# Graph attention on one core: other run lengths at attention's end, second parts in the step in which a run ends, and one-hot matrices of the last 60 chunks on ScalarE

## The chip, the cores and the metric

The kernel runs on one core of one Trainium2 chip, as one launch. The metric is device time in microseconds (us): the median over several executions. Beside it there is one execution taken by the hardware profiler, which has its own time. The engines are named as the profile names them: PE is TensorE (PEld its weight loads), DVE is VectorE, ACT is ScalarE, POOL is GpSimd, SP is SyncE, which here only issues DMAs.

## What is computed

A graph of 6250 nodes with 128 features and 200,000 edges, sorted by their destination. A layer norm and a rectifier, two convolutions over the edges, and then one attention over the edges, whose part is what the change touches:

```python
q = (h @ qw + qb).reshape(n, H, HD)          # H = 8 heads, HD = 16
k = (h @ kw + kb).reshape(n, H, HD)
v = (h @ vw + vb).reshape(n, H, HD)
logits = (q[dst] * k[src]).sum(-1) * scale + (edge_attr @ ew + eb)
amax = jax.ops.segment_max(logits, dst, num_segments=n)
pe = jnp.exp(logits - amax[dst])
ssum = jax.ops.segment_sum(pe, dst, num_segments=n)
w = pe / jnp.clip(ssum[dst], 1e-06)
o = jax.ops.segment_sum(w[:, :, None] * v[src], dst, num_segments=n)
o = group_norm(o.reshape(n, D) @ ow + ob, an_g, an_b)
return h + o
```

## The kernel before

**Chunks and stages.** The edges are worked in 196 chunks (`NCH`) of 8 tiles (`TPC`) of 128 edges; the last chunk has 3 tiles. The stages follow each other: a preparation, convolution 1, convolution 2, attention, and the last nodes. The change is in attention, and in `pipeline`, `early` and `second`, which the convolutions share; for them it changes only signatures.

**A chunk's first part.** `fetch` issues the loads: on SP's queue 112 rows of the table of queries into `pk` (L634) and, for two chunks at a time, the edges' relative destinations and attributes into `ohT` (L618, L621); on GpSimd's queue 8 indirect gathers (L648) of keys and values into `g`, one of 11 buffers. ScalarE turns `ohT` into a transposed one-hot matrix with a Square and a Relu (`compared`, L643 and L644). `products` multiplies it with `pk` on TensorE, 8 matmuls into `qe` (L1237), of which there is one buffer. `logits` multiplies `qe` with the gathered keys on VectorE (L1252, into `g`), reduces over each head (L1256) and adds the edges' part (L1258), which ScalarE has copied out of `qe` (L1254).

**A run.** Some chunks in a row are a run. At its end `maxima` finds the largest logit of each destination: `load_runs` has brought masks `nbs` and `nbe`, one DMA per chunk each (L1267), TensorE transposes the logits of the whole run (L1283), VectorE scans them forward and backward (L1286, L1287), TensorE transposes the result back (L1291), VectorE subtracts (L1295), ScalarE takes the exponent (L1297), and VectorE makes weights for the later maximum (L1299). `maxima` is a generator: it stops twice, so that other work stands between its pieces.

**A chunk's second part** needs its run's maxima. `onehot` compares the destinations with 0 to 127 on VectorE (L654) into `oh`, one of two buffers. `add_late` adds what the chunk before the last summed to the table (L1335 to L1341). `weighted` multiplies values and weights (L1309, the last use of the chunk's `g`) after ScalarE's copies (L1308, L1414, L1415). `sums` multiplies with the one-hot on TensorE (L1316, into one of two `us`). `merge_late` then takes up the sums of the chunk before (L1349 to L1327 on VectorE, two exponents L1329 and L1331 on ScalarE).

**Steps.** `spread` gives the lengths of the runs and `steps_of` says in which step each chunk's second part stands. In attention runs are of 8 chunks, and the last four of 6, 4, 1 and 1; a run's second parts become due in the step after the one in which it ends and are spread over the steps until the next ones are due, one or two in each. `pipeline` writes a step in this order: fetch of chunk n + 2, then `second` (with the maxima of a run that ends here between the parts of it), then `first` (the logits of chunk n), the rest of `maxima`, `compared` of chunk n + 2, `products` of chunk n + 1, `early`, and one piece of each batch of node work that is under way. Such a batch of four windows of nodes starts every 8 steps (`attention_nodes`, with rows on each engine in some 10 steps). `in_order` then fixes this order on VectorE, ScalarE, TensorE and SP; no scheduler changes it. Step 195 is the last with logits; before the change steps 196 and 197 hold the rest.

**What follows from the buffers.** With 11 buffers of `g`, the gather of chunk c + 11 waits until L1309 of chunk c is done. In runs of 8 the second part of chunk n - 9 stands in step n.

Of the kernel before, what the change touches and what calls it, by code (L numbers as in the profile page):

```python
# [8 lines left out]
FP = mybir.dt.float32  # L9
BF = mybir.dt.bfloat16  # L10
I32 = mybir.dt.int32
AF = mybir.ActivationFunctionType
ALU = mybir.AluOpType
AX = mybir.AxisListType
DVE = mybir.EngineType.DVE
# [6 lines left out]
P = 128  # L22
# [10 lines left out]
LG = 2  # L33
WN = 112
SOON = 24
KE = 5
KW = WN + KE
DB = D + H
# [9 lines left out]
def kernel(ctx: ExitStack, tc: tile.TileContext, x, src, dst, eat, w, out):  # L48
# [293 lines left out]

    def spread(i):

        sizes, n = ([1, 1, 4, 6], G) if i == 3 else ([GC] + [1] * 4, GC)
        rest, out = NCH, []
        while rest:
            out.insert(0, min(rest, sizes.pop(0) if sizes else n))
            rest -= out[0]
        return out  # L350

    def steps_of(i):


        ends, due, n = {}, {}, 0
        for m in spread(i):
            ends[n + m] = list(range(n, n + m))
            due.setdefault(n + m + (i == 3 or n < NCH - SOON), []).extend(ends[n + m])
            n += m
        waiting, todo, left = [], [], NCH  # L360
        while left:
            n = len(todo)
            waiting += due.get(n, ())
            steps = min([m for m in due if m > n], default=n + 1) - n
            k = -(-len(waiting) // steps)
            todo.append(waiting[:k])
            waiting = waiting[k:]
            left -= k
        return ends, todo
# [372 lines left out]
    def pipeline(i, stage, aside=iter(())):  # L742

        start = len(nc.cur_bb.bb.instructions)
        ends, todo = steps_of(i)  # L750
        starts = {n: j for j, (n, _) in enumerate(plans[i])}
        ahead = stage.ahead
        ks, under_way = {}, []
        for c in range(ahead):
            ks[c] = stage.fetch(c)
            compared(ks[c])
        stage.products(ks[0])
        for n, seconds in enumerate(todo):
            if n + ahead < NCH:
                ks[n + ahead] = stage.fetch(n + ahead)  # L760
            if n + 1 < NCH and stage.soon:
                stage.products(ks[n + 1])
            run = [ks[c] for c in ends.get(n, ())]
            stage.root(run)
            if n + ahead < NCH and stage.soon:
                compared(ks[n + ahead])
            stage.second(run, [ks.pop(c) for c in seconds])
            if n < NCH:
                stage.first(ks[n])
            stage.finish()  # L770
            if n + ahead < NCH and not stage.soon:
                compared(ks[n + ahead])
            if n + 1 < NCH and not stage.soon:
                stage.products(ks[n + 1])
            if n < NCH:
                stage.early(ks, n)
            if n in starts:
                for _ in aside:
                    pass
                under_way.append(stage.batch(starts[n]))  # L780
            for g in list(under_way):
                if next(g, STOP) is STOP:
                    under_way.remove(g)
            if n > 4:
                next(aside, None)
            if n < NCH:
                stage.reduce(ks[n])
        stage.flush()
        for g in (*under_way, aside):
            for _ in g:  # L790
                pass
        in_order(start)
# [111 lines left out]
    def attention_nodes(b, w, m):  # L904
# [15 lines left out]
            nc.sync.dma_start(out=hx[1][:TAIL, whole, :], in_=x[FULL * P:N, :])  # L920
        yield
        tT = b.turned(st, m)
        yield
        o = b.times(tT, m, squares["ow"])
        yield
        A = b.tile(m, "A")
# [29 lines left out]
    def with_root(b, batch):  # L956

        var = b.pool.tile([P, BN * H], FP, name="n_var")
        b.var = lambda: var
        for r in batch:  # L960
            yield
            if r == "root":
                yield from own_root(b, var, BN * H)

# [33 lines left out]
    def conv(i):  # L998
# [4 lines left out]
        with ExitStack() as es:  # L1003
# [74 lines left out]
            class Stage:  # L1078
# [23 lines left out]
                def reduce(self, k):  # L1102
                    k.reduce()

                def early(self, ks, n):

                    for k in [ks[c] for c in sorted(ks) if c <= n and ks[c].oh is None][:1]:
                        if n == NCH - 1 or k.c <= self.next:
                            onehot(k, pools, iota)
# [4 lines left out]
                        self.sd = deviations(n, self.var, NV + BN * H - n if self.roots else 0)  # L1114
                        self.j = 0

                def second(self, run, ks):
                    if run and ks and run[0].c <= ks[-1].c:
                        self.inverse(run)
                        run = []  # L1120
                    for k in ks:
                        self.next = k.c + 1
                        if k.oh is None:
                            onehot(k, pools, iota)
                        if self.late:
                            add_late(self.late.pop(0))
                        normed(k)
                        summed(k)
                        if self.sums:
                            by_window(self.sums[0])  # L1130
                            self.late.append(self.sums.pop())
                        self.sums.append(k)
                    self.inverse(run)

                def inverse(self, run):
                    if run:
# [68 lines left out]
    with ExitStack() as es:  # L1205
# [11 lines left out]
        def iota_of(k):  # L1217
            return us[k.c % 2][:, IO:IO + D // 2].bitcast(BF)
# [41 lines left out]
        def load_runs(run, bp):  # L1260

            nb = {}
            for name, d_ in (("nbs", nbs_d), ("nbe", nbe_d)):
                nb[name] = bp.tile([G * H, EPC], BF, name=name)
                for j, c in enumerate(run):
                    n = min(TPC, EI - c * TPC)
                    nc.sync.dma_start(  # L1267
                        out=nb[name][j * H:(j + 1) * H, :n * P],
                        in_=d_[c * TPC:c * TPC + n, :].rearrange("t p -> (t p)")[None, :].to_broadcast([H, n * P]))
            return nb  # L1270

        def maxima(run, lg, nb, bp):
# [83 lines left out]
        def add_late(k):  # L1356
            add(k, t3[:, bass.ds(k.win, 2), :], 2)

        class Stage:
            ahead, soon = 2, False  # L1360
            sums, late, nb = [], [], None
# [16 lines left out]
            def first(self, k):  # L1378
                if self.j == 0:
                    self.lg = wk.tile([P, TPC, G, H], FP, name="lg")  # L1380
                logits(k, self.lg[:, :, self.j, :])
                self.j += 1

            def reduce(self, k):
                pass

            def early(self, ks, n):
                pass

            def root(self, run):  # L1390
                if self.nb is None and self.runs:
                    self.nb = load_runs(self.runs.pop(0), self.bp)

            def second(self, run, ks):


                pieces = iter(())
                if run:
                    pieces = maxima(run, self.lg, self.nb, self.bp)
                    self.nb, self.j = None, 0  # L1400
                for n, k in enumerate(ks):
                    mine = pieces if n == len(ks) - 1 else iter(())
                    next(mine, None)
                    onehot(k, pools, iota_of(k))
                    if self.sums:
                        self.sums[0].win = value(w0_i, self.sums[0].c, DVE, NW - 1)
                    next(mine, None)
# [11 lines left out]
                        self.late.append(self.sums.pop())  # L1419
                    self.sums.append(k)  # L1420
                self.pieces = pieces

            def finish(self):
                for _ in self.pieces:
# [99 lines left out]
```

## Time and profile before

| what | value |
|---|---|
| median of 3 runs (lowest, highest) | 8048.32 us (8045.71, 8068.07) |
| the profiled execution: time, span | 8041.9 us, 8040.2 us |
| mean granted clock of TensorE | 0.68 |
| VectorE, GpSimd, TensorE, ScalarE busy, share of the span | 63%, 56%, 50%, 41% |
| attention: first and last start of the reduction L1256 | 5114.7, 7995.2 us |
| last add of attention ends; span ends | 8013.3, 8040.2 us |

A group's line names the source line, engine, operation, tiles written and read and count; after the bar stand busy us, the mean ns of one, then the engine's idle time just before those instructions and what ended most of it. A timeline line has the start in us, the duration, the engine, the line, the operation and the tiles; in brackets the idle time before it and what ended it. "remote" is a wait whose releaser the records don't name, "issue" is time in which the engine waited for nothing that they show.

### The profile page before, as it was taken

The numbers are of one execution on the slowest core, as the hardware profiler recorded it, in microseconds if no ns is written. First come the engines' busy times: TensorE is split into PE (matmuls) and PEld (weight loads), VectorE is DVE, ScalarE is ACT, GpSimd is POOL, SyncE is SP. The second block draws the span as 40 slices with busy tenths as digits, with TensorE's granted clock in tenths as the row PEclk, the third lists the DMA queues.
The fourth block names the chain that finished last, engine by engine and source line by source line (L and its number), as shares of the span: only waits on it lengthen the run. The fifth ranks groups of instructions, "written<-read, shape, count | busy, mean of one in ns | idle before, by whom it ended". The sixth has DMA issues, their size and how long they took to land. (4 is left out here: it accounts for less than half of the span.)

```text
span 8040.2 us, 71956 instructions
## 1 busy us (share of the span) xinstructions
PE 4000.1 (50%) x20903; PEld 3683.9 (46%) x20904; DVE 5083.1 (63%) x7387; ACT 3300.5 (41%) x5103; POOL 4484.0 (56%) x4703
## 2 busy tenths in 40 slices
PE   4555554545544454555545554254545555545544
PEld 4444444444544444445544443244444444444444
DVE  5666766666655566666766665355556556655657
ACT  4555555555544455555555544222222222222222
POOL 5666666656653666666665654445555545555552
PEclk7776667776666666766777766666666666666666
DMA  4433333333322333333333332344443444434442
GB/s 131 112 90 92 89 101 90 91 89 90 90 77 62 87 92 82 93 92 92 97 95 95 96 94 72 94 115 117 115 121 114 116 115 121 117 111 122 121 117 64
DMA packets 413748, 798.12 MB, mean 99 GB/s; under 512 B 101571, under 2 KB 274758, under 8 KB 379285
## 3 DMA queue, kind: packets, MB, share of 16 engines
q0 software_dynamic: 175056, 410.03, 19.0%
q1 hardware_dynamic: 232644, 379.76, 16.4%
q10 hardware_dynamic: 5632, 3.50, 0.2%
q8 instruction: 173, 2.83, 0.2%
q14 instruction: 243, 1.99, 0.1%
HBM read 751.94 MB, written 40.96 MB: 99 GB/s over the span
## 5 line engine op out<-in xcount | busy, mean ns | idle before, releaser
L648 POOL DMA_INDIRECT g<-b_d,src_i x3126 | 2974.6, 952 | 1931.7 <-DVE h L1041 970.1
L648 POOL DMA_INDIRECT g<-kv_d,src_i x1563 | 1488.8, 953 | 1355.0 <-DVE cm L1352 795.5
L1066 PE MATMUL u<-h,oh 128*128 128x129 f32 (+1 forms) x6252 | 1320.6, 381 | 1663.3 <-ACT h L1061 864.5
L1066 PEld LDWEIGHTS u<-h,oh 128*128 128x128 f32 x6252 | 1190.6, 285 | 1773.9 <-ACT h L1061 902.1
L1034 PE MATMUL m<-pk,ohT 117*128 117x128 f32 x6252 | 1093.3, 326 | 765.0 <-issue 722.0
L1034 PEld LDWEIGHTS m<-pk,ohT 117*128 117x128 f32 x6252 | 1008.6, 241 | 828.1 <-issue 783.4
L1041 DVE TENSOR_TENSOR h<-m,g 128x1024 f32<-128x1024 f32 x392 | 475.3, 1212 | 1058.4 <-remote 975.7
L1316 PE MATMUL us<-v,oh 128*128 128x145 f32 x3126 | 720.1, 398 | 630.4 <-issue 328.0
L1237 PE MATMUL qe<-pk,ohT 117*128 117x136 f32 x3126 | 624.6, 370 | 679.6 <-issue 394.4
L1316 PEld LDWEIGHTS us<-v,oh 128*128 128x128 f32 x3126 | 644.6, 281 | 694.2 <-issue 693.9
L1237 PEld LDWEIGHTS qe<-pk,ohT 117*128 117x128 f32 x3126 | 578.2, 271 | 726.4 <-issue 460.0
L643 ACT ACTIVATE ohT<-ohT,minus_p 112x1024 f32<-112x1024 f32 x588 | 670.5, 1140 | 35.1 <-DMA ohT<-rel_d 23.4
L1061 ACT ACTIVATE h<-h 128x1024 f32<-128x1024 f32 x392 | 412.8, 1053 | 587.7 <-DVE h L1060 292.2
L1071 ACT ACTIVATE u<-u,mask 128x129 f32<-128x129 f32 (+1 forms) x784 | 264.0, 337 | 926.5 <-remote 850.6
L644 ACT ACTIVATE ohT<-ohT 112x1024 f32<-112x1024 f32 x588 | 619.7, 1054 | 18.6
L1252 DVE TENSOR_TENSOR g<-qe,g 128x768 f32<-128x768 f32 (+1 forms) x391 | 251.8, 685 | 564.7 <-remote 439.9
L1045 DVE TENSOR_REDUCE var<-sq 128x64 f32<-128x1024 f32 x392 | 475.0, 1212 | 133.3 <-ACT u L1071 55.7
L654 DVE TENSOR_TENSOR oh<-cps,dm 128x1024 f32<-128x1024 f32 x392 | 474.4, 1210 | 96.4 <-remote 95.2
L1059 DVE TENSOR_TENSOR h<-h,cps 128x1024 f32<-128x1024 f32 x392 | 477.1, 1217 | 13.5
L1060 DVE TENSOR_TENSOR h<-h,cps 128x1024 f32<-128x1024 f32 x392 | 477.1, 1217 | 13.4
L1043 ACT ACTIVATE sq<-h 128x1024 f32<-128x1024 f32 x392 | 411.3, 1049 | 166.0 <-DVE h L1041 139.3
L1056 DVE TENSOR_TENSOR h<-h,cps 128x1024 f32<-128x1024 f32 x392 | 474.0, 1209 | 0.0
(272 smaller groups left out, 4066.4 us busy)
## 6 DMA issues: line engine op xcount, KB each, us to landing
ohT<-rel_d SPq DMA_DIRECT2D x291, 896.0 KB
g<-b_d,src_i POOLq DMA_INDIRECT x3126
pk<-a_d SPq DMA_DIRECT2D x588, 56.0 KB
g<-kv_d,src_i POOLq DMA_INDIRECT x1563
ohT<-in_eat_dram SPq DMA_DIRECT2D x291, 40.0 KB
a_d<-n_o SPq DMA_DIRECT2D x28, 256.0 KB
kv_d<-n_o SPq DMA_DIRECT2D x28, 256.0 KB
n_h<-h_d SPq DMA_DIRECT2D x19, 256.0 KB
```

The costliest lines, as they stand in the source:

```text
L643: nc.scalar.activation(k.ohT[:WN, :], k.ohT[:WN, :], AF.Square, bias=minus_p[:WN])
L644: nc.scalar.activation(k.ohT[:WN, :], k.ohT[:WN, :], AF.Relu, bias=1.0, scale=-4.0)
L648: nc.gpsimd.indirect_dma_start(out=g[:, t, :table_d.shape[1]], out_offset=None, in_=table_d, in_offset=bass.IndirectOffsetOnAxis(ap=k.src[ ...
L654: return nc.vector.tensor_tensor(k.oh[:, :k.nt, :], iota[:, None, :].to_broadcast([P, k.nt, P]), k.dm[:, :, None].to_broadcast([P, k.nt, P ...
L1034: nc.tensor.matmul(k.m[:, t, :], lhsT=lhs[:, t * P:(t + 1) * P], rhs=rhs, start=(j == 0), stop=(j == len(terms) - 1))
L1041: nc.vector.tensor_tensor(k.mt, k.m[:, :n], k.g[:, :n], ALU.add)
L1045: return lambda: nc.vector.tensor_reduce(var[:, at:at + n * H], sq[:, :n].rearrange("p t (g c) -> p (t g) c", c=HD), AX.X, ALU.add)
L1059: nc.vector.tensor_tensor(k.mt, k.mt, over_edges(gam, k.nt), ALU.mult)
L1060: nc.vector.tensor_tensor(k.mt, k.mt, over_edges(bet, k.nt), ALU.add)
L1066: nc.tensor.matmul(k.u[:, 0, :wide], lhsT=k.oh[:, t, :], rhs=k.h[:, t, :wide], start=(t == 0), stop=(t == k.nt - 1))
L1237: nc.tensor.matmul(k.qe[:, t // TB, at:at + DB], lhsT=lhs[:, t * P:(t + 1) * P], rhs=rhs, start=(j == 0), stop=(j == len(terms) - 1))
L1316: nc.tensor.matmul(k.u[:, :wide], lhsT=k.oh[:, t, :], rhs=k.v[:, t, :wide], start=(t == 0), stop=(t == k.nt - 1))
```

## The change

The last seven runs of attention become 7, 7, 6, 5, 4, 3 and 4 chunks (`TAILS`). `spread` takes the list from its back, so that 4 is the last, and 160 chunks in 20 runs of 8 stand before them. Second parts of these 36 chunks become due in the step in which their run ends instead of the one after. So steps 161 and 162 hold two second parts, and so do 174, 180 and 185, where a run ends; step 189 holds two, step 195 none and step 196 the last four; step 197 is gone. Where a run's own second parts stand in its last step (`own`), `second` writes another order: the transposes, the one-hot of the run's second chunk that stands here, the logits of chunk n (`first`), the late add, all the rest of `maxima`, and then the second parts.

For the last 60 chunks (`BY_ACT`) `early` lets ScalarE make the one-hot of the next step's first second part, as 1 - (j - d) squared, cut off below zero: 8 Squares with a bias from the destinations and one Relu (`onehot_by_act`). With the one in `own` that is 56 chunks; of the other four (153, 155, 194, 195) VectorE still makes it. VectorE's count of L654 in attention goes from 196 to 140; ScalarE gets 56 x 9 instructions.

A batch of nodes stops once with "held": if a run ends in the next step, its piece waits one step. The masks' loads are now always of a whole chunk, and a short chunk's unused logits are set to zero. The diff:

```diff
--- before.py
+++ after.py
@@ -33,6 +33,8 @@
 LG = 2
 WN = 112
 SOON = 24
+TAILS = [7, 7, 6, 5, 4, 3, 4]
+BY_ACT = 60
 KE = 5
 KW = WN + KE
 DB = D + H
@@ -342,7 +344,7 @@
 
     def spread(i):
 
-        sizes, n = ([1, 1, 4, 6], G) if i == 3 else ([GC] + [1] * 4, GC)
+        sizes, n = (TAILS[::-1], G) if i == 3 else ([GC] + [1] * 4, GC)
         rest, out = NCH, []
         while rest:
             out.insert(0, min(rest, sizes.pop(0) if sizes else n))
@@ -355,7 +357,7 @@
         ends, due, n = {}, {}, 0
         for m in spread(i):
             ends[n + m] = list(range(n, n + m))
-            due.setdefault(n + m + (i == 3 or n < NCH - SOON), []).extend(ends[n + m])
+            due.setdefault(n + m + (n < NCH - (sum(TAILS) if i == 3 else SOON)), []).extend(ends[n + m])
             n += m
         waiting, todo, left = [], [], NCH
         while left:
@@ -750,7 +752,7 @@
         ends, todo = steps_of(i)
         starts = {n: j for j, (n, _) in enumerate(plans[i])}
         ahead = stage.ahead
-        ks, under_way = {}, []
+        ks, under_way, said = {}, [], {}
         for c in range(ahead):
             ks[c] = stage.fetch(c)
             compared(ks[c])
@@ -764,22 +766,25 @@
             stage.root(run)
             if n + ahead < NCH and stage.soon:
                 compared(ks[n + ahead])
-            stage.second(run, [ks.pop(c) for c in seconds])
-            if n < NCH:
-                stage.first(ks[n])
+            first = (lambda k: lambda: stage.first(k))(ks[n]) if n < NCH else None
+            if stage.second(run, [ks.pop(c) for c in seconds], first) and first:
+                first()
             stage.finish()
             if n + ahead < NCH and not stage.soon:
                 compared(ks[n + ahead])
             if n + 1 < NCH and not stage.soon:
                 stage.products(ks[n + 1])
             if n < NCH:
-                stage.early(ks, n)
+                stage.early(ks, n, todo[n + 1])
             if n in starts:
                 for _ in aside:
                     pass
                 under_way.append(stage.batch(starts[n]))
             for g in list(under_way):
-                if next(g, STOP) is STOP:
+                if said.get(g) == "held" and n + 1 in ends:
+                    continue
+                said[g] = next(g, STOP)
+                if said[g] is STOP:
                     under_way.remove(g)
             if n > 4:
                 next(aside, None)
@@ -920,7 +925,7 @@
             nc.sync.dma_start(out=hx[1][:TAIL, whole, :], in_=x[FULL * P:N, :])
         yield
         tT = b.turned(st, m)
-        yield
+        yield "held"
         o = b.times(tT, m, squares["ow"])
         yield
         A = b.tile(m, "A")
@@ -958,7 +963,7 @@
         var = b.pool.tile([P, BN * H], FP, name="n_var")
         b.var = lambda: var
         for r in batch:
-            yield
+            yield r
             if r == "root":
                 yield from own_root(b, var, BN * H)
 
@@ -1102,7 +1107,7 @@
                 def reduce(self, k):
                     k.reduce()
 
-                def early(self, ks, n):
+                def early(self, ks, n, then):
 
                     for k in [ks[c] for c in sorted(ks) if c <= n and ks[c].oh is None][:1]:
                         if n == NCH - 1 or k.c <= self.next:
@@ -1114,7 +1119,7 @@
                         self.sd = deviations(n, self.var, NV + BN * H - n if self.roots else 0)
                         self.j = 0
 
-                def second(self, run, ks):
+                def second(self, run, ks, first):
                     if run and ks and run[0].c <= ks[-1].c:
                         self.inverse(run)
                         run = []
@@ -1131,6 +1136,7 @@
                             self.late.append(self.sums.pop())
                         self.sums.append(k)
                     self.inverse(run)
+                    return True
 
                 def inverse(self, run):
                     if run:
@@ -1263,10 +1269,9 @@
             for name, d_ in (("nbs", nbs_d), ("nbe", nbe_d)):
                 nb[name] = bp.tile([G * H, EPC], BF, name=name)
                 for j, c in enumerate(run):
-                    n = min(TPC, EI - c * TPC)
                     nc.sync.dma_start(
-                        out=nb[name][j * H:(j + 1) * H, :n * P],
-                        in_=d_[c * TPC:c * TPC + n, :].rearrange("t p -> (t p)")[None, :].to_broadcast([H, n * P]))
+                        out=nb[name][j * H:(j + 1) * H, :],
+                        in_=d_[c * TPC:(c + 1) * TPC, :].rearrange("t p -> (t p)")[None, :].to_broadcast([H, EPC]))
             return nb
 
         def maxima(run, lg, nb, bp):
@@ -1356,6 +1361,12 @@
         def add_late(k):
             add(k, t3[:, bass.ds(k.win, 2), :], 2)
 
+        def onehot_by_act(k):
+            k.oh = pools["oh"].tile([P, TPC, P], FP, name="oh")
+            for t in range(k.nt):
+                nc.scalar.activation(k.oh[:, t, :], iota_j, AF.Square, bias=k.dm[:, t:t + 1], scale=-1.0)
+            nc.scalar.activation(k.oh[:, :k.nt, :], k.oh[:, :k.nt, :], AF.Relu, bias=1.0, scale=-1.0)
+
         class Stage:
             ahead, soon = 2, False
             sums, late, nb = [], [], None
@@ -1378,30 +1389,48 @@
             def first(self, k):
                 if self.j == 0:
                     self.lg = wk.tile([P, TPC, G, H], FP, name="lg")
+                if k.nt < TPC:
+                    nc.vector.memset(self.lg[:, k.nt:, self.j, :], 0.0)
                 logits(k, self.lg[:, :, self.j, :])
                 self.j += 1
 
             def reduce(self, k):
                 pass
 
-            def early(self, ks, n):
-                pass
+            def early(self, ks, n, then):
+
+                if then and then[0] >= NCH - BY_ACT:
+                    onehot_by_act(ks[then[0]])
 
             def root(self, run):
                 if self.nb is None and self.runs:
                     self.nb = load_runs(self.runs.pop(0), self.bp)
 
-            def second(self, run, ks):
+            def second(self, run, ks, first):
 
 
                 pieces = iter(())
                 if run:
                     pieces = maxima(run, self.lg, self.nb, self.bp)
                     self.nb, self.j = None, 0
+                own = bool(run and ks and ks[0] is run[0])
+                if own:
+                    next(pieces, None)
+                    for k in ks[1:2]:
+                        onehot_by_act(k)
+                    if first:
+                        first()
+                    if self.sums:
+                        self.sums[0].win = value(w0_i, self.sums[0].c, DVE, NW - 1)
+                    if self.late:
+                        add_late(self.late.pop(0))
+                    for _ in pieces:
+                        pass
                 for n, k in enumerate(ks):
                     mine = pieces if n == len(ks) - 1 else iter(())
                     next(mine, None)
-                    onehot(k, pools, iota_of(k))
+                    if k.oh is None:
+                        onehot(k, pools, iota_of(k))
                     if self.sums:
                         self.sums[0].win = value(w0_i, self.sums[0].c, DVE, NW - 1)
                     next(mine, None)
@@ -1419,6 +1448,7 @@
                         self.late.append(self.sums.pop())
                     self.sums.append(k)
                 self.pieces = pieces
+                return not own
 
             def finish(self):
                 for _ in self.pieces:
```

## The prediction

> **What bounds the kernel now.** I read the page's busy shares first, then its costliest groups, then the stretches of 200 us, the waits, and the timeline of single steps; the page's chain of waits ends in the last DMAs within a few us and says nothing about the steps. No engine is full: VectorE is busy 63% of the span, GpSimd 56%. The change touches only attention's last 36 to 60 chunks, so I read there.
>
> ```profile
> 7600.00:7800.00 200.00, 105.71 (x519) 97.59 (x519) 125.89 (x263) 48.87 (x137) 108.34 (x115) 0.67 0.44 123
> 7800.00:8040.00 240.00, 107.40 (x564) 99.04 (x562) 164.71 (x394) 51.89 (x165) 67.97 (x72) 0.69 0.25 70
> ```
>
> The columns are busy us (instructions) of TensorE, its weight loads, VectorE, ScalarE and GpSimd, then clock, DMA share and GB/s. Up to 7800 VectorE has a third of its time free; at the end it has little. The groups:
>
> ```profile
> L648 POOL DMA_INDIRECT g<-kv_d,src_i x1563 | 1488.8, 953 | 1355.0 <-DVE cm L1352 795.5 <-issue 470.6 <-DVE v L1309 48.8
> ...
> L654 DVE TENSOR_TENSOR oh<-us,dm 128x1024 f32<-128x1024 bf16 x196 | 237.6, 1212 | 2.0 <-ACT us L1329 1.4
> ```
>
> A gather takes 0.95 us and the next follows 0.30 later, so a chunk's eight take 10.0 us. They stand idle until VectorE has finished with a buffer (the releaser named is the step just after L1309, the last reader of `g`). The one-hot costs VectorE 1.21 us, 1.14 from start to start. Steps come every 14.2 us between chunks 160 and 184 (the reduction L1256 starts at 7457.5 and 7797.7), and most of what isn't work is this:
>
> ```profile
> 7045.10 1.22 DVE L1309 TENSOR_TENSOR v<-g,pe 128x1024 f32<-128x1024 f32 x1
> ...
> 7055.53 0.94 POOL L648 DMA_INDIRECT g<-kv_d,src_i  x1 [0.30 <-issue]
> ...
> 7056.96 0.40 PE L1316 MATMUL us<-v,oh 128*128 128x145 f32 x1 [2.40 <-issue]
> ...
> 7060.52 0.16 DVE L1349 SCALAR_TENSOR_TENSOR nm<-us,nm 128x2 f32<-128x2 f32 x1 [14.21 <-remote]
> ```
>
> While gathers run, TensorE's matmuls come 0.7 to 2.8 us apart instead of 0.24, and VectorE waits 14.2 us for a sum. The wait ends 3 to 4 us after the burst's last gather, and so do most long waits in this stage. VectorE then works through a step to the next L1309, which frees a buffer and starts the next burst. The path from the end of a stall to that L1309 is what the change can shorten or stretch. Who sets it is read from one step:
>
> ```profile
> 7029.84 1.06 ACT L644 ACTIVATE ohT<-ohT 112x1024 f32<-112x1024 f32 x1
> ...
> 7030.81 0.25 ACT L1308 COPY v<-pe 128x64 f32<-128x64 f32 x1
> ...
> 7031.23 1.22 DVE L654 TENSOR_TENSOR oh<-us,dm 128x1024 f32<-128x1024 bf16 x1
> ...
> 7033.86 1.22 DVE L1309 TENSOR_TENSOR v<-g,pe 128x1024 f32<-128x1024 f32 x1
> ```
>
> L1309 also needs ScalarE's copy L1308, done at 7031.06: ScalarE has 2.8 us of slack here. Over the steps that end no run the slack goes 0.03, 1.2, 1.5, 2.8, 3.1, 3.9 us as node work comes and goes.
>
> **The change, part by part.**
>
> One-hots, steps 145 to 160. Of the last 60 chunks, 56 get theirs from ScalarE: eight Squares of 128x128 and a Relu of 128x1024. The nearest row for a Square with a per-partition bias is a square root of that size:
>
> ```profile
> L1052 ACT ACTIVATE sd<-var,eps_t 128x128 f32<-128x128 f32 x162 | 65.1, 402 | 49.4 <-DVE var L1045 27.1 <-issue 20.7
> ```
>
> Neighbours on ScalarE overlap by 0.09, so 8 x 0.31 + 0.09 + 1.06 (row L644) = 3.6 us. From below, the one bare Square of this size took 0.316, so 8 x 0.22 + 1.06 = 2.8; from above, with no overlap, 8 x 0.40 + 1.06 = 4.3. I take 3.6, whose row has the same kind of bias. It stands in ScalarE's order between L644 and L1308, so L1309 moves by the larger of -1.14 and 3.6 less the slack (less, too, ScalarE's own waiting before a node copy). Over chunks 136 to 151 that sums to +17 us for all sixteen; counting only the L1309s that start a burst, since a stall hides the others, it is +6. I take +6. VectorE's 16 x 1.14 = 18 us disappears into the same waits. If the cover goes, it is the +17.
>
> ScalarE: Activation LUTs of the Trainium skill, section Rules for kernel authors, says to give relu and arithmetic to VectorE rather than ScalarE; the rows agree in direction (1.21 against about 3.6 us), and by the rule alone this part would be a loss in every step, which is a rival below.
>
> Gather stretch, steps 161 to 188. Before, 468 us pass from 7457.5 to the end of the last gather at 7925.8, in step 191. After, second parts come in their run's own step, two at a time in 161, 162, 174, 180 and 185, and the last gather's buffer comes free in step 188: 27.5 steps instead of 30.5. A step is 14.2. What a doubled second part and its gather cost is in the trace: 7797.7 to 7925.8 is 128 us for 6.5 steps (92) and three extra second parts, 12 each. So 27 x 14.2 + 5 x 12 = 443. A run that ends in its own step (167, 174, 180, 185) puts in a row what was spread: logits 2.8, late add 1.5, scans 4.6, transposes back 1.3, subtraction 0.6, exponent 0.6, copy 0.3 = 11.7 us to its first L1309, against 7.8 now (7786.45 to 7794.23): 4 x 3.9 = 15. One-hots by the rule above, bursts only: 10. Sum 468: no change. SP issues the same loads of `nbs` and `nbe` in other steps; it is idle for most of each, and the scans come more than 7 us after them. TensorE's order changes only where runs end, and node batches wait there one step; the matmuls are the same.
>
> The drain. From the first merge after the last gather (7928.35) to the last add (8013.3) VectorE has 85.0 us almost without a gap:
>
> ```profile
> 7972.14 1.21 DVE L1309 TENSOR_TENSOR v<-g,pe 128x1024 f32<-128x1024 f32 x1
> ...
> 7977.07 1.22 DVE L1309 TENSOR_TENSOR v<-g,pe 128x1024 f32<-128x1024 f32 x1
> ```
>
> A second part is 4.93 us; without its one-hot 3.79. After, the drain begins three steps earlier and holds eight logits (7 x 2.8 + 1.4 = 21), eleven second parts (nine at 3.79, one at 4.93, the short last one 4.0: 43), three pairs of scans (13.7), subtractions and weights (3.5), a node batch (6.4) and the last merges (4.7): 92 us. Then waits that were not there. With VectorE at 2.8 + 3.79 = 6.6 a step, ScalarE's way from one L1309 to the next is longer: to the merge 1.1, to L1252 1.1, to L1254 1.4, the rows to L1308 2.3, one-hot 3.6, copy 0.3 = 9.8. That is 3.2 in steps 190 and 191, 2 in 193, 1 in 194: 9. Three runs that end wait 1.6 each for TensorE and the exponent: 5. In 189 and 192 the logits follow the last logits directly and wait for products (about 4 us from L1254) and for L1254 behind one or two one-hots: 6 + 3. Node work fills some 3. Sum 92 + 20 = 112, or +27; without those waits it would be +7.
>
> Together 6 + 0 + 27 = +33 on the profiled run's own 8041.9 us (span 8040.2 and 1.7 around it): **8075 us**. The median of the runs shown is 6.4 above that run, within their spread, and I don't add it.
>
> **Rivals.**
>
> *The gathers' lead is free* (faster). Buffers come free up to three steps sooner; GpSimd is idle some 135 of the 468 us, and if the extra gathers go there without stretching TensorE's stalls, an extra second part costs VectorE's 3.8 instead of 12. Then 27 x 14.2 + 19 + 15 = 417, -51; with the one-hots hidden in the stalls (0) and the drain at +27 it is -24: 8018 us. If the drain's waits are covered too, 8000. It decides once an extra second part costs less than about 5 us. For it: GpSimd's waits name VectorE. Against it: in the doubled step 185 VectorE waited 19.6 us behind a burst of three chunks.
>
> SBUF — State Buffer of the Trainium skill, section Who interferes with whom, says that a DMA never contends with a compute engine and that TensorE shares its ports with nobody; by that this rival is right. The trace speaks against it: of 451 matmul gaps over 0.6 us inside groups, 421 fell while gather packets moved.
>
> *ScalarE sets every step* (slower still). If no stall hides the later L1309s, steps 145 to 160 cost +17 and the gather stretch 12 more: +56, 8098 us; with the upper price of a one-hot 8115. For it: slack of 0.03 us in every eighth step and in the node-copy steps. Against it: L1309s within a burst have gathers queued in front of them.
>
> *It cancels.* The shorter stretch pays for the drain, 8030 to 8055. That the change doesn't do what it says can be left out: the changed kernel's order of instructions has 56 one-hots on ScalarE and the runs as named.
>
> **How the numbers follow.** The forecast has 0.42 and its own range is 8050 to 8098; the free lead has 0.30, ScalarE in every step 0.16, cancelling 0.12. From 8005 to 8110 leaves out the ends of both outer rivals. Under 0.3%, 24 us, a measurement of this kernel can hardly be told from no change. Slower (over 8072): 0.27 of the forecast, 0.16 of the third case, 0.43 in all. Faster (under 8024): 0.21 of the free lead, 0.03 of its neighbour, 0.24. The rest, 0.33, lies between.
>
> **What would show it.** Right: a drain of 105 to 118 us after the last gather, with VectorE waiting for L1308 at L1309 and for L1254 at L1258; the Square near 0.40 us, the pieces of a one-hot 3.6; the last gather within 15 us of 7926 plus 6; steps 145 to 160 a few us longer. Wrong: the last gather before 7890, a drain under 95, waits at L1309 that ScalarE does not end, or bursts of four and five chunks without longer stalls.

## The result and the profile after

The changed kernel takes 8082.96 us (median of 13 runs, 8054.44 to 8097.87) against 8052.67 for the kernel before in the same set (13 runs, 8029.24 to 8077.29): 1.0035 times as long, 95% interval 1.002 to 1.0049. The forecast was 8075 us. Run again later (e12) it was 1.0023, 1.0008 to 1.0039. The profiled run took 8089.8 us, of which the span is 8088.0.

Two stretches first, with the columns of the prediction (busy us and instructions of TensorE, its weight loads, VectorE, ScalarE and GpSimd; clock, DMA share, GB/s):

```profile
7600.00:7800.00 200.00, 85.49 (x421) 77.89 (x422) 101.02 (x232) 88.36 (x242) 94.25 (x100) 0.64 0.37 107
7800.00:8040.00 240.00, 110.08 (x602) 103.38 (x601) 134.16 (x308) 114.09 (x316) 78.30 (x82) 0.68 0.27 78
```

ScalarE's work has about doubled (48.87 to 88.36 us in the first, 51.89 to 114.09 in the second), VectorE's has fallen (125.89 to 101.02), and GpSimd issues 100 gathers in the first stretch where it issued 115. Groups (busy us and mean ns of one, then idle time before them and what ended it):

```profile
L650 POOL DMA_INDIRECT g<-kv_d,src_i x1563 | 1485.7, 951 | 1398.0 <-DVE cm L1357 828.3 <-issue 445.1 <-DVE v L1314 56.1
...
L1367 ACT ACTIVATE oh<-iota_j,dm 128x128 f32<-128x128 f32 x448 | 136.1, 386 | 0.0
L1368 ACT ACTIVATE oh<-oh 128x1024 f32<-128x1024 f32 x56 | 59.2, 1056 | 1.8
...
L1314 DVE TENSOR_TENSOR v<-g,pe 128x1024 f32<-128x1024 f32 x196 | 237.5, 1212 | 134.8 <-ACT v L1313 108.3 <-issue 25.4
```

The weighting, L1309 before, is L1314 now. Before, its group was this:

```profile
L1309 DVE TENSOR_TENSOR v<-g,pe 128x1024 f32<-128x1024 f32 x196 | 236.8, 1208 | 51.2 <-ACT v L1308 49.2 <-issue 0.3
```

It waits 108 us for ScalarE instead of 49. The Square is 0.386 us, and GpSimd stands idle 43 us longer before attention's gathers (1355.0 to 1398.0). Where the time went, from the starts of the logits' reductions (L1256, now L1262), the last gather's end and the last add's end in the two traces:

| | before | after | difference | forecast |
|---|---|---|---|---|
| start to chunk 144 | 7225.0 | 7233.4 | +8.4 | 0 |
| chunks 144 to 160 | 232.5 | 217.9 | -14.6 | +6 |
| chunk 160 to last gather | 468.4 | 495.8 | +27.4 | 0 |
| drain, to the last add | 87.5 | 114.6 | +27.1 | +27 |
| rest | 26.8 | 26.4 | -0.4 | 0 |

(The prediction counted before's drain from its first merge, 85.0 us; from the last gather's end it is 87.5.) The spans differ by 47.8 us and the medians by 30.3, so the differences hold some chance: the +8.4 ahead of chunk 144 is made of an attention that begins 18 us earlier and takes 27 longer to that chunk, where the only change is the waiting node batch (see e2). The sum came close; two of its three terms didn't. One step of the gather stretch, from the second part of a run that ends in its own step (timeline: start, us, engine, line; in brackets idle time and releaser):

```profile
7687.97 1.22 DVE L1314 TENSOR_TENSOR v<-g,pe 128x1024 f32<-128x1024 f32 x1
...
7689.46 0.94 POOL L650 DMA_INDIRECT g<-kv_d,src_i  x1 [18.16 <-DVE cm L1357]
...
7692.05 1.22 DVE L1314 TENSOR_TENSOR v<-g,pe 128x1024 f32<-128x1024 f32 x1
...
7700.12 1.22 DVE L1314 TENSOR_TENSOR v<-g,pe 128x1024 f32<-128x1024 f32 x1 [3.90 <-ACT v L1313]
...
7716.23 0.40 PE L1321 MATMUL us<-v,oh 128*128 128x145 f32 x1 [1.70 <-issue]
...
7718.20 0.95 POOL L650 DMA_INDIRECT g<-kv_d,src_i  x1 [0.30 <-issue]
7718.33 0.40 PE L1321 MATMUL us<-v,oh 128*128 128x145 f32 x1 [1.70 <-issue]
7723.27 1.29 DVE L1258 TENSOR_TENSOR g<-qe,g 128x768 f32<-128x768 f32 x2 [20.78 <-remote]
...
7732.68 0.94 POOL L650 DMA_INDIRECT g<-kv_d,src_i  x1 [13.54 <-DVE cm L1357]
```

GpSimd waits 18 us until the run's first weighting, three weightings then release three chunks, their 24 gathers stand in one burst to 7719, TensorE's matmuls come mostly 2.1 us apart, and VectorE waits 20.8 us, to 4 us after the burst. There are 265 gathers in this stretch in both kernels, 328 us with the 0.30 between them; GpSimd's idle gaps over 0.6 us sum to 139.7 us before and 167.7 after, 16 gaps in each.

### The profile page after: what moved, and what is told of

Its sections match the earlier page's. It is cut to its first block, busy times and chain, and to the rows that moved or that the text cites. A ratio compares the mean times of both kernels' runs of the same rounds, so it can differ in the third digit from the quotient of the medians.

```text
span 8088.0 us, 72425 instructions
## 1 busy us (share of the span) xinstructions
PE 3991.9 (49%) x20913; PEld 3669.4 (45%) x20914; DVE 5029.4 (62%) x7337; ACT 3488.4 (43%) x5607; POOL 4472.4 (55%) x4703
## 5 line engine op out<-in xcount | busy, mean ns | idle before, releaser
L650 POOL DMA_INDIRECT g<-kv_d,src_i x1563 | 1485.7, 951 | 1398.0 <-DVE cm L1357 828.3
L1071 PE MATMUL u<-h,oh 128*128 128x129 f32 (+1 forms) x6252 | 1337.3, 384 | 1723.0 <-ACT h L1066 897.0
L1243 PE MATMUL qe<-pk,ohT 117*128 117x136 f32 x3126 | 586.4, 353 | 432.9 <-issue 238.6
L1243 PEld LDWEIGHTS qe<-pk,ohT 117*128 117x128 f32 x3126 | 545.9, 257 | 471.2 <-issue 275.3
L645 ACT ACTIVATE ohT<-ohT,minus_p 112x1024 f32<-112x1024 f32 x588 | 670.5, 1140 | 47.7 <-DMA ohT<-rel_d 30.3
L1334 ACT ACTIVATE us<-d 128x16 f32<-128x16 f32 x196 | 36.7, 187 | 1067.5 <-DVE d L1331 782.0
```

Source lines behind the costliest of these rows:

```text
L645: nc.scalar.activation(k.ohT[:WN, :], k.ohT[:WN, :], AF.Square, bias=minus_p[:WN])
L650: nc.gpsimd.indirect_dma_start(out=g[:, t, :table_d.shape[1]], out_offset=None, in_=table_d, in_offset=bass.IndirectOffsetOnAxis(ap=k.src[ ...
L1071: nc.tensor.matmul(k.u[:, 0, :wide], lhsT=k.oh[:, t, :], rhs=k.h[:, t, :wide], start=(t == 0), stop=(t == k.nt - 1))
L1243: nc.tensor.matmul(k.qe[:, t // TB, at:at + DB], lhsT=lhs[:, t * P:(t + 1) * P], rhs=rhs, start=(j == 0), stop=(j == len(terms) - 1))
```

## The experiments

The experiments fell on four chips (that of the first set of runs isn't on record): e1 to e4 on one, e5 to e8 on a second, e9 and e10 on a third, e11 and e12 on a fourth. On the second the kernel before takes 6172 us, on the others 8038 to 8067; each ratio is against the kernel before in the same set of runs. "Run of 8" is the time between the logits of two chunks 8 apart in attention. Kernels with before's runs are the changed file with the lines shown put back; its `memset` for the short chunk and its loads of `nbs` and `nbe` at full width stay in them.

**e1: one-hots on ScalarE in all chunks, nothing else changed.** `onehot_by_act` as in the diff, with before's runs and steps:

```diff
-BY_ACT = 60
+BY_ACT = 196
...
-        sizes, n = (TAILS[::-1], G) if i == 3 else ([GC] + [1] * 4, GC)
+        sizes, n = ([1, 1, 4, 6], G) if i == 3 else ([GC] + [1] * 4, GC)
...
-            due.setdefault(n + m + (n < NCH - (sum(TAILS) if i == 3 else SOON)), []).extend(ends[n + m])
+            due.setdefault(n + m + (i == 3 or n < NCH - SOON), []).extend(ends[n + m])
...
-                if said.get(g) == "held" and n + 1 in ends:
+                if False:
```

> Kernel before's runs and due steps, node batches not held, but ScalarE makes the one-hots of all 196 chunks instead of VectorE. By the prediction a one-hot on ScalarE delays the L1309s that start a burst of gathers, +6 us for 16 chunks: 12 times that, about 8050 + 74 = 8125 us; if no stall hides the others, +17 for 16, about 8260. The rival comes from the trace of the changed kernel: its runs of 8 without ScalarE's one-hots last 119 to 120 us and its two runs of 8 with them 105 and 112. If that is their doing, each of some 23 runs of 8 gains 5 to 14 us over before (111 to 121): 7730 to 7930 us.

7906.35 us against 8066.71: 0.98, 0.9783 to 0.9817. It is the fastest of the versions that gather in all chunks, and the forecast's sign for the one-hots is wrong. Runs of 8 from chunk 48 on take 104 to 113 us. In a run of 8 of this kernel, the gathers that a named releaser let go (GpSimd's timeline):

```profile
6916.49 0.94 POOL L650 DMA_INDIRECT g<-kv_d,src_i  x1 [11.64 <-DVE cm L1357]
...
6928.67 0.94 POOL L650 DMA_INDIRECT g<-kv_d,src_i  x1 [2.46 <-DVE cm L1357]
...
6951.19 0.95 POOL L650 DMA_INDIRECT g<-kv_d,src_i  x1 [1.45 <-DVE v L1314]
...
6971.87 0.95 POOL L650 DMA_INDIRECT g<-kv_d,src_i  x1 [10.95 <-DVE cm L1357]
...
6997.27 0.95 POOL L650 DMA_INDIRECT g<-kv_d,src_i  x1 [5.52 <-DVE nm L1354]
```

Bursts of 8, 8, 8, 8, 16 and 16 gathers (the third, not shown, starts at 6940.0), with breaks of 1.5 to 2.5 us between the short ones.

**e2: only the waiting node batch.** Against e1's kernel, with before's runs and steps:

```diff
-BY_ACT = 196
+BY_ACT = 0
...
-                if False:
+                if said.get(g) == "held" and n + 1 in ends:
```

> Kernel before with one edit: a node batch in attention isn't advanced at the end of the step before a run ends, once it has been turned. The prediction gave that no cost: 8040 to 8065 us, and runs of 8 of both 112 and 120 us as before. The rival: the changed kernel's twelve runs of 8 from chunk 48 to 144 all last 119 to 120 us, while seven of before's last 120 and five 112 to 114; if the waiting batch does that, all are near 120 here and the time is about 20 us longer, 8065 to 8080.

8061.3 against 8066.71 us: 1.0002, 0.9992 to 1.0013. The time is as the prediction had it. The runs of 8 are as the rival had them, all 118 to 120 us, chunks 48 to 144 in 1432.9 us. So all runs near 120 cost nothing against the kernel before on this chip; the short runs in before's first profile (four of the twelve, 112 to 114 us, where the expectation counts five) were probably a chance of that execution (e11, with before's code and no holding, has 119 to 120 in the five whole runs that it gathers from chunk 48 to 160), but a second profile of before on such a chip is missing. One run of 8 of e2:

```profile
6963.73 0.94 POOL L650 DMA_INDIRECT g<-kv_d,src_i  x1 [10.73 <-DVE cm L1357]
...
7008.35 0.94 POOL L650 DMA_INDIRECT g<-kv_d,src_i  x1 [14.92 <-DVE nm L1354]
...
7052.27 0.94 POOL L650 DMA_INDIRECT g<-kv_d,src_i  x1 [13.82 <-DVE cm L1357]
...
7084.08 0.94 POOL L650 DMA_INDIRECT g<-kv_d,src_i  x1 [12.11 <-DVE nm L1354]
```

Bursts of 24, 24 and 16 gathers, each followed by a gap of 12 to 15 us: about 40 us of idle time in a run, where e1 has 25 to 34. From chunk 48 to 144, 20 of e2's 39 bursts are of 24 gathers and 3 of 8; in e1 3 of 64 are of 24 and 34 of 8.

**e3: the changed kernel with VectorE's one-hots.**

```diff
-BY_ACT = 60
+BY_ACT = 0
...
-                        onehot_by_act(k)
+                        onehot(k, pools, iota_of(k))
```

> The changed kernel with every one-hot on VectorE; runs, own steps and held batches stay. By the prediction it loses the one-hots' +6 in steps 145 to 160, +10 in the stretch and some 5 to 9 us of waits in the drain, which VectorE's 9 x 1.14 us more than half gives back: 8083 - 20 = about 8063 us. The rival, that one-hots on ScalarE shorten steps (105 and 112 us for the runs of 8 that have them against 120): these two runs go back to 120 each, 8083 + 23 - 5 = about 8100 us.

8086.83 against 8066.71 us: 1.0025, 1.0012 to 1.0037, between the two expectations and not to be told from the changed kernel by time. By parts: chunks 144 to 160 take 238.8 us (217.9 with ScalarE, 212.3 in e12), chunk 160 to the last gather 487.6 (495.8 and 484.5), the drain 108.1 (114.6 in both). The one-hots on ScalarE gain some 24 us in the two runs of 8 and lose 6.5 in the drain, by these profiles; the times don't show the net gain.

**e4: the same last runs, second parts one step later.**

```diff
-            due.setdefault(n + m + (n < NCH - (sum(TAILS) if i == 3 else SOON)), []).extend(ends[n + m])
+            due.setdefault(n + m + (i == 3 or n < NCH - SOON), []).extend(ends[n + m])
```

> The changed kernel with the same last runs, but their second parts from the step after the one in which a run ends, as before the change: no second part of a run in its own step, doubled second parts in 161, 175, 181, 186 and 190. If the own step is what costs the gather stretch its 28 us (three steps of 47 to 49 us after chunks 174, 180 and 185), the stretch from chunk 160 to the last gather shrinks by about 20 to 30 us, to 465 to 475, though the last buffer comes free one step later (+14); the drain stays within 10 us of 115. Sum: 8060 to 8085 us. If bursts of three chunks are what costs, whatever step they start in, the stretch stays at 490 or above and the time at 8080 to 8110.

8059.14 us: 0.9996, 0.9983 to 1.0009. The stretch to the last gather is 482.0 us, not 465 to 475, the drain 101.9, where the expectation had 105 to 125: 584 us for both together against 610 in the changed kernel (599 in e12). By these profiles starting second parts in the run's own step costs 15 to 26 us; the steps of 47 to 49 us are gone, and the largest is 28.

**e5: both engines make the one-hots.** e1's kernel, in which VectorE makes a one-hot of its own for each chunk, in the other of the two buffers `oh`, and ScalarE's is thrown away:

```diff
-                    if k.oh is None:
-                        onehot(k, pools, iota_of(k))
+                    onehot(k, pools, iota_of(k))
```

> Kernel before's runs; ScalarE makes all 196 one-hots as in e1 and they are thrown away, for VectorE makes them as well, as before. VectorE keeps all of its work and gets ScalarE's wait on top. If e1 gained because VectorE has 1.14 us less in each step, this run is slower than before: 8066 and up to 17 us for every 16 chunks more, 8070 to 8270 us. If it gained because ScalarE's way from one weighting to the next (11.3 us) is longer than a chunk's gathers (10.0), so that a burst ends after each chunk and TensorE catches up in the gap, this run keeps most of the gain: runs of 8 of 105 to 113 us, 7900 to 7960 us.

**e6: breaks between gathers, e7: no gathers in 64 chunks, e8: before again.** e6 and e7 are before, each with one edit in attention's `fetch` (`rest` in e6 is a scratch tile):

```diff
                 gather(k, k.g, kv_d)
+                for _ in range(8):
+                    nc.gpsimd.memset(rest, 0.0)
```

> Kernel before, and GpSimd writes a scratch tile eight times (about 2 us in all) after the gathers of each attention chunk; VectorE and ScalarE work as before. If short breaks between the chunks' gathers let TensorE through, runs of 8 shrink from 112 to 121 us to 105 to 113 and the time to 7880 to 8000 us, although GpSimd has some 390 us more to do. If GpSimd's gathers set the pace, the 2 us are added to most chunks: 8100 to 8450 us.

```diff
-                gather(k, k.g, kv_d)
+                if 64 <= c < 128:
+                    nc.sync.dma_start(out=k.g, in_=kv_d[:TPC * P, :].rearrange("(t p) c -> p t c", p=P))
+                else:
+                    gather(k, k.g, kv_d)
```

> Kernel before with chunks 64 to 127 of attention filled by one direct transfer each from SyncE's queue (the first 1024 rows of the table, the same number of bytes) instead of eight gathers by GpSimd, so that other numbers come out. If GpSimd's gathers are what makes TensorE late, TensorE's gaps over 0.6 us all but go in these chunks, VectorE has no wait over 10 us, and a run of 8 there takes 75 to 95 us against 112 to 121 for the others. If any transfer into SBUF does it, or the low clock alone, the gaps and the waits stay and a run of 8 stays at 105 or above.

> Kernel before, unchanged, for a second profile of it. Its first has runs of 8 of 112 to 114 us (five of the twelve from chunk 48 to 144) and of 120 to 121. If that mix is chance, the second has another mix and its stretch from chunk 48 to 144 differs from 1414 us by a multiple of about 7; if it is fixed by the node batches, the same runs are short again and it lies within 3 us.

On this chip before takes 6171.61 us (7 runs, 6169.9 to 6173.74), and the thing in dispute isn't there, so none of the four tested what it should. A stretch of e8's attention:

```profile
4400.00:4900.00 500.00, 303.48 (x1731) 285.07 (x1731) 423.51 (x912) 169.96 (x476) 378.43 (x400) 0.80 0.63 169
```

VectorE is busy 85%, a run of 8 takes 79 to 84 us (chunks 48 to 144) and attention's gathers have no gap over 0.6 us. The 400 gathers, one every 1.25 us, fill the 500 us: here GpSimd's queue sets the pace. Of 1516 intervals between matmuls of one sum at clock 0.5 with gathers under way, one is over 0.6 us. e5 is 1.0187 (1.017 to 1.0204): here ScalarE's wait costs 5 to 6 us in each run of 8 and gives nothing. e7 has 73 to 75 us a run in its altered chunks. e6 took 6606.33 us and shows nothing: the 1568 writes ran from 901 to 1937 us, long before attention, where the program's order had pulled them.

**e9 and e10: e5 and e1 once more,** on a third chip, where before takes 8038.3 us.

> The kernel of e5, once more, because e5 to e8 ran on a chip on which the kernel before takes 6172 us and no matmul comes late. If before takes about 8060 us here: VectorE's relief as the cause of e1's gain gives 8070 to 8270 us, the wait for ScalarE as a pace that splits bursts gives runs of 8 of 105 to 113 us and 7900 to 7960 us. If before takes about 6170 us here too, it repeats e5: 1.019 of before.

> The kernel of e1, once more. If before takes about 8060 us here: 0.98 of it, as in e1. If before takes about 6170 us: no bursts of gathers end in a stall there, so pacing has nothing to give; ScalarE's way of 11.3 us (e5: runs of 8 of 85 to 86 us against 79 to 84) stays in each step, and the 1.14 us of VectorE are behind it. By that 1.01 to 1.02 of before, 6235 to 6295 us; if VectorE's relief counts, 0.97 to 0.99.

e10 is 7992.29 us, 0.9932 (0.9905 to 0.996); less than e1's gain, the same sign. e9 is 7999.25 us, 0.9955 (0.9933 to 0.9976): VectorE does all that it did before and waits for ScalarE on top, and the kernel is faster. The time lies between the two ranges expected; its runs of 8, 111 to 113 us from chunk 48 to 144, are as the pace would have them. Its gathers:

```profile
6958.76 0.95 POOL L650 DMA_INDIRECT g<-kv_d,src_i  x1 [12.25 <-DVE cm L1357]
...
6970.92 0.95 POOL L650 DMA_INDIRECT g<-kv_d,src_i  x1 [2.45 <-DVE cm L1357]
...
6982.21 0.95 POOL L650 DMA_INDIRECT g<-kv_d,src_i  x1 [1.55 <-DVE v L1314]
...
6998.22 0.95 POOL L650 DMA_INDIRECT g<-kv_d,src_i  x1 [6.30 <-DVE cm L1357]
```

Bursts of 8, 8, 8 and 16, as in e1. At clock 0.5 with gathers under way, intervals over 0.6 us between matmuls of one group (sums and products) are 349 of 2286 in e2, 97 of 3155 in e10 and 55 of 3115 in e9. In e9 47 of 72 bursts from chunk 48 to 144 are of 8 gathers and none of 24. So the gain doesn't need VectorE's relief; later weightings are enough. I read it as a pace: a weighting every 11.3 us releases the next chunk just after the last one's 10.0 us of gathers, and TensorE gets through before the next burst.

ScalarE isn't all that delays e9. With two one-hots per chunk in two buffers, VectorE's has to wait until TensorE has summed the chunk before. That wait stood at the merge (L1354) in e2, is far shorter in e9, and comes before the weighting there; e2's line first, then e9's:

```profile
L1354 DVE SCALAR_TENSOR_TENSOR nm<-us,nm 128x2 f32<-128x2 f32 x196 | 30.1, 153 | 680.1 <-remote 676.8 <-issue 3.0 <-PE us L1321 0.3
```

```profile
L656 DVE TENSOR_TENSOR oh<-us,dm 128x1024 f32<-128x1024 bf16 x196 | 238.8, 1218 | 188.5 <-remote 155.8 <-issue 18.9 <-PE us L1321 7.4
```

No run sets the breaks between gathers alone (e6 was to), so that the bursts are the link is argued from their counts. What VectorE's 1.14 us per chunk add can't be told: e9's and e10's intervals overlap.

**e11 and e12: e7 and the changed kernel once more,** on a fourth chip, where before takes 8067.16 us.

> The kernel of e7, once more (chunks 64 to 127 of attention are filled by one direct transfer each from the table's first 1024 rows, so other numbers come out). Where before takes about 8050 us: if GpSimd's gathers make TensorE late, its gaps over 0.6 us all but go in these chunks though the clock stands at 0.5 as often, and a run of 8 falls from 112 to 121 us to 75 to 95. If the low clock alone does it, or any transfer into SBUF, gaps stay and a run of 8 stays over 105. Where before takes about 6170 us it repeats e7: 74 us a run.

> The changed kernel, unchanged. Where before takes about 8050 us: 1.0035 of it, the ten runs of 8 before chunk 144 at 119 to 120 us again, three steps of 47 to 49 us after chunks 174, 180 and 185. Where before takes about 6170 us: no late sums, so the own steps and doubled second parts cost what VectorE does in them alone; from chunk 144 on steps wait for ScalarE's 11.3 us against 10.0 (85 to 86 a run, +5 for each of six), and the drain keeps its +27 or less: 1.006 to 1.009 of before, 6210 to 6230 us.

e11 is 0.9545 (0.9525 to 0.9565), from 64 of 196 chunks. Windows of its direct chunks and of chunks 132 to 160, which are gathered:

```profile
6023.10:6550.00 526.90, 329.56 (x2014) 313.39 (x2012) 491.45 (x1068) 205.72 (x554) 0.00 (x0) 0.83 0.65 186
6679.60:7104.50 424.90, 210.36 (x1010) 186.93 (x1009) 246.33 (x521) 100.82 (x272) 214.00 (x226) 0.64 0.41 113
```

Without gathers VectorE is busy 93% of the time, with them 58%; more bytes move without them (186 against 113 GB/s). The granted clock is higher too, 0.83 against 0.64, which the expectation didn't have; but at 0.5 none of the first window's 553 intervals between matmuls of one group is over 0.6 us, and 71 of 482 in the second are, so the low clock alone doesn't do it. The group that waits for a sum, in the same two windows:

```profile
L1354 DVE SCALAR_TENSOR_TENSOR nm<-us,nm 128x2 f32<-128x2 f32 x56 | 8.4, 151 | 0.0
```

```profile
L1354 DVE SCALAR_TENSOR_TENSOR nm<-us,nm 128x2 f32<-128x2 f32 x28 | 4.3, 152 | 106.9 <-remote 106.9
```

No wait at all against 106.9 us in 28. A run of 8 takes 73 to 75 us in whole altered runs, as on the second chip, and 119 to 120 with gathers. So GpSimd's gathers, not transfers into SBUF as such, hold TensorE up. Whether it matters who issues them or which rows they read, e11 doesn't separate: its direct transfers read 1024 rows in order. e12 repeats the result: steps of 41, 49, 48 and 47 us at 162, 175, 181 and 186 (41, 49, 47 and 47 the first time), a drain of 114.6.

## Why the prediction was right, and where it was not

**What bounds the kernel** was right: TensorE's results come late while gathers run, and e11 shows it by taking the gathers away. The argument for it was weaker than it looked: 421 of 451 long gaps under gather packets is a count, and gathers follow each other every 1.25 us through 68% of attention. Rates say it (the last section has them). SBUF — State Buffer of the Trainium skill, section Who interferes with whom, says that a DMA never contends with a compute engine. On e8's chip, with one long interval in 1516, the traces agree, and so do e11's direct transfers; with gathers on the three other chips they do not.

**Steps 145 to 160, +6: wrong in sign.** The prices held. A Square is 0.386 us, the eight 2.43 to 2.45, with the Relu of 1.06 about 3.5 where 3.6 was taken, and L1314 waits for ScalarE as said (4.2 us at 7253 and 7359). The step that failed is "L1309 moves by the larger of -1.14 and 3.6 less the slack", summed over the L1309s that start a burst, with the bursts taken as given. A later L1309 changes the bursts. Three profiles with VectorE's one-hots and eight-chunk runs (before, e2, e11) have 232.5, 238.9 and 238.3 us for these two runs; after, e12 and e4, with ScalarE's, 217.9, 212.3 and 210.2: some 23 us less, and e9 shows that waiting alone splits the bursts. From chunk 48 to 144, 33 of e2's 36 bursts of 16 or more gathers are followed by a gap of 10 to 15 us, and 27 of e1's 34 bursts of 8 by one under 3.

ScalarE: Activation LUTs of the Trainium skill, section Rules for kernel authors, gives relu to VectorE, which would have made this a loss in every step. The price agrees (3.5 us against 1.21), but e1 and e10, at 0.98 and 0.9932, go against the loss; e5, at 1.0187 on the chip without late sums, goes with it for the wait that it causes.

**Gather stretch, 0: too low.** Against before's own profile it is +27 us (+16 in e12); against the mean of the three profiles with before's runs, 468.4, 477.8 and 485.7, it is +13 for the mean of after and e12. The undersized terms are "5 doubled second parts x 12" and "4 x 3.9" for a run that ends in its own step: each of the three steps that have both was to take about 14 + 12 + 4 = 30 us and takes 47 to 49, with one gap of 12 to 18 us ahead of the run's first weighting and a second of 13 behind the burst of three chunks. e4 tells the two terms apart: there a doubled step and the one behind it take 37 to 47 us (steps 175, 181 and 186), some 15 more than two steps of 14.2, where 12 was taken; in the changed kernel these pairs take 57 to 59, so the own step adds about 15 more, where 3.9 was taken. The other steps pay part of it back: the 24 steps that remain of 161 to 188, without those three and 162, average 12.9 us, not 14.2.

**Drain, +27: right,** in its parts too. The waits:

```profile
DVE v L1314 <- ACT v L1313: 13.8, 4, 4.4
DVE lg L1264 <- ACT ebs L1260: 3.9, 2, 2.4
DVE lg L1300 <- PE blk L1296: 3.6, 3, 1.2
DVE g L1258 <- PE qe L1243: 1.8, 2, 1.4
```

(us in total, times, longest.) VectorE's idle time in the drain is 31.1 us against 9.0 before: 22 of the 27 are new waits, 17.7 of them for L1313 and L1260 as named; 20 were forecast. Of the 27, ScalarE's one-hots make only 6.5 by e3, which has 108.1 us: 15.3 us of waits less and 8.8 of VectorE's own one-hots more. The other 20.6 stay without them: 6.8 of waits and 13.8 of work in a drain that begins three steps earlier.

**The sum.** By the mean of after and e12 against the three profiles: -22 + 13 + 27 = +18 us; the times say +30 and +20. The forecast +6 + 0 + 27 = +33 got there with two errors of opposite sign; that it came so close is luck. The rival with ScalarE in every step (8098) fails by e1; the free lead (8018) by the bursts of three chunks, which stall VectorE 15 to 21 us; cancelling by the stretch, which grew: the gain of the two runs of 8 (-22) pays for it (+13), but not for the drain.

## What to carry to other kernels

Where one engine's work and a queue's transfers hamper each other, a wait can't be priced with the queue's bursts held fixed: work out first what the new release times do to the bursts. A longer path on a helper engine may pace them and win 0.5 to 2%, and releasing three buffers at once may lose what an earlier release should gain. Look at the idle gaps of the queue (their number, and the size of the burst before each), not only at the waits of the busiest engine, and try the suspected pace with the relieved work put back, as e9 does.

## What the runs showed of the hardware

Chips differ far more than the change: the same program took 6172 us on one and 8038 to 8067 on three others. On those three TensorE's lateness needs the low clock and gathers together. The granted clock has two levels in all traces, 0.5 and 1.0, and holds each for a multiple of about 3.4 us. TensorE: Matmul & The Clock Gate of the Trainium skill, section Part 1: The HAM clock gate, says the same of the levels and the window. Round the stall shown above, in the changed kernel:

```profile
7689.00:7702.00 13.00, 9.16 (x60) 8.84 (x61) 7.58 (x26) 6.83 (x21) 9.50 (x11) 0.87 0.31 91
...
7706.00:7710.00 4.00, 0.53 (x2) 0.36 (x2) 0.00 (x0) 0.00 (x0) 3.09 (x4) 0.50 0.40 108
7710.00:7714.00 4.00, 0.81 (x2) 0.79 (x3) 0.00 (x0) 0.00 (x0) 3.09 (x4) 0.50 0.38 114
...
7723.20:7727.00 3.80, 2.03 (x9) 2.03 (x10) 3.59 (x6) 2.32 (x5) 0.00 (x0) 0.50 0.77 239
```

The same gathers at 0.87 let 60 matmuls through in 13 us, at 0.50 two in 4; once they are over, nine in 3.8 us at the same 0.50. In the changed kernel 15% of the intervals between matmuls of one sum are over 0.6 us at 0.5 with gathers (248 of 1649), 0.3% at 1.0 with gathers (3 of 921); an interval goes by the clock at its second matmul, and gathers count until some 2 us after the last issue. On the chip of 6172 us the level 0.5 is there too, with gathers, and no sum comes late. What differs between the chips, and by which way gathers reach TensorE, no run here tells. The changed kernel and e1 were not run on that chip; e5 lets one expect a loss from ScalarE's wait there.
